# Attention that divides by sums standing on 16 rows of each head, without transposes

## The chip, the cores and the metric

The kernel runs on one core of one Trainium2 chip, as one launch. The metric is device time in microseconds (us); the time of a version is the median of its runs. The profile shows one execution of the program, taken by the hardware profiler.

## What is computed

The inputs are `x` and a context `ctx_1024`, each 8 batches x 256 tokens x 256 columns, float32. Four layers follow each other, each added to `x`:

```
x = x + autocorrelation_attention(layernorm(x), ctx, ctx)     # layer 0
x = x + expert_mlp_balanced(layernorm(x))                     # layer 0, 8 experts
x = x + cross_attention(layernorm(x), ctx)                    # layer 1
x = x + expert_mlp_top2(layernorm(x))                         # layer 1, 8 experts, 8 shared
```

The change is in the cross attention of layer 1, with 16 heads of 16 columns:

```
q  = (x @ Wq + bq).reshape(bs, n_ctx, 16, 16)
kv = (data @ Wkv + bkv).reshape(bs, n_data, 16, 32);  k, v = kv[..., :16], kv[..., 16:]
attn = softmax(einsum('bqhd,bkhd->bhqk', q, k) / 4, axis=-1)
out  = einsum('bhqk,bkhd->bqhd', attn, v).reshape(bs, n_ctx, 256) @ Wp + bp
```

The last layer's shared and routed experts are three products each, with a gate `silu(x @ w1) * (x @ w3)` and `@ w2`.

## The kernel before

The order of the instructions on each engine is the order of the Python code (a manual schedule); the engines run beside each other and meet at semaphores that the tile framework sets from the tiles' reads and writes. A tile of a pool with n buffers waits for the release of the tile n allocations earlier in the same pool and tag. PSUM has eight banks of 2 KB per row (512 float32).

`fast_path` holds the whole computation (a general path follows only if a flag is set). Its stages by the profile: layer 0 with its search for balanced experts and its products until about 214 us, the cross attention until about 343 us, overlapped at its end with the first block of the shared experts, then the expert blocks to the end.

**Before the attention.** `keys` and `vals` project the context. `vals` (L1414 to L1428) leaves the values in `VA`, 32 columns per head: 16 of values, then a column of ones and 15 of zeros, set by two POOL memsets (L1496, L1497). At L2467 to L2474 the rows of the output weights `wp` and of the value bias `bvc` are loaded in the order in which the heads will stand.

**The attention loop** (from L3019 on) goes over the 8 batches `b`, two steps `c` each; a step covers 8 heads, `4 g x 2 m`. In a step `scores(b, c, kt)` (L2666) makes, for each of two blocks `kt` of 128 keys, four 32-row matmuls over 512 columns into two tiles of `ps_s` (two banks each), and ScalarE writes the exponential to SBUF (L2681). `values` (L2685) of the step before multiplies `VA` with the exponentials: for each `g` and `m` a product of 32 rows (16 of values, one of sums) into `ps_v`, one bank, `[128, 2, 256]`. Then:

- `keep` (L2698) copies that bank to SBUF, `ov`, on VectorE.
- `turn_back(b)` (L2702) transposes `ov` back to tokens x columns on TensorE, 8 transposes a batch, takes the reciprocal of the sums, now one column per head, and multiplies: `on`.
- `turn_out(b)` (L2724) transposes `on` again, 4 transposes, and VectorE copies them to `oT`, the stationary operand of `project_out` (L2737).

Beside this run for other batches: `turn_q` (4 transposes of the normalised `x`, copied to `hT`), `queries` (L2633: products and two masked copies `QM`, one on ScalarE and one on VectorE), `add_y`, `batch_stats`, `norm_q`, `norm_m` (statistics on VectorE, their last steps on POOL), `take_apart_m` and `join_m` (ScalarE, with DMA transposes), and from batch 4 on `route`, the router of 512 tokens in eight pieces (L2844), whose small matmuls (logits `pl`, L2849; a transpose; counts behind `mk`, L2898 to L2903) use `ps_m`, and whose VectorE part is some thirty small operations. `send` issues the routed rows' indirect DMAs on POOL.

PSUM in this stage: `ps_m` three banks (transposes, queries, projection, router), `ps_s` two tiles of two banks, `ps_v` one bank.

**Behind the loop** (L3767 on) the last batch's `turn_back`, `turn_out` and `project_out` stand between the pieces of `classic_up` (the first block of the shared experts, L3248 to L3258) and of `route(2)`. At L3828 the banks are closed and new pools opened for the expert blocks: `Bs` two banks, `ps_a` two, `ps_e` two, `ps_m` and `ps_v` one each. `run_unit` then makes seven products per block with lists of VectorE steps (`early`, `amid`, `late`, `after`) put between them; `Rows.steps()` are four sums of the block's rows that the products need (tile `T`).

Of the kernel before, what the change touches and what calls it, by code (L numbers as in the profile page):

```python
# [9 lines left out]
F32 = mybir.dt.float32  # L10
BF16 = mybir.dt.bfloat16
U32, U16 = mybir.dt.uint32, mybir.dt.uint16
# [1074 lines left out]
def fast_path(  # L1087
# [261 lines left out]


    KT = pk.tile([P, NB, T], F32, name="KT")
    VA = pk.tile([P, NT, H, HW], F32, name="VA")
    WK = pst.tile([P, KC, H, DH], F32, name="WK")
    wkv = wkv_in.rearrange("p kc (h t d) -> p kc h t d", h=H, t=2)
    mask = pk.tile([P, 2], F32, name="mask")
# [59 lines left out]
    def vals(i, n, pool, copy=nc.scalar.copy):  # L1415
        pp = pool.tile([P, n, H, DH], F32, tag="pm", name="pp")
        for j in range(n):
            for kc in range(KC):
                nc.tensor.matmul(
                    pp[:, j],  # L1420
                    CT[:, kc, (i + j) * P : (i + j + 1) * P],
                    wkv[:, kc, :, 1, :],
                    start=(kc == 0),
                    stop=(kc == KC - 1),
                )
                if kc < KC - 1 or j < n - 1:
                    yield
        copy(VA[:, i : i + n, :, 0:DH], pp)  # L1428
        yield

    def in_steps(steps, n):
# [61 lines left out]
    )  # L1493
    bsel = pr.tile([P, NCT, 16], F32, name="bsel")
    nc.vector.tensor_copy(bsel, fold.to_broadcast([P, NCT, 16]))
    nc.gpsimd.memset(VA[:, :, :, DH:], 0.0)  # L1496
    nc.gpsimd.memset(VA[:, :, :, DH : DH + 1], 1.0)  # L1497

    spread = pa.tile([P, 2, 8, DH], F32, name="spread")
    nc.gpsimd.tensor_copy(  # L1500
# [963 lines left out]
    for e in range(E - 1):  # L2464
        if e == 5:

            wpv = L1_xattn_Wp.rearrange("(c g m d) n -> m g d c n", c=NB, g=4, m=2)  # L2467
            for m in range(2):
                for g in range(4):
                    r0 = 64 * m + DH * g  # L2470
                    nc.sync.dma_start(out=wp[r0 : r0 + DH], in_=wpv[m, g])
                    nc.sync.dma_start(
                        out=bvc[r0 : r0 + DH, :],
                        in_=bkv[:, 1, :].rearrange("(c g m) d -> m g d c", c=NB, g=4)[m, g],  # L2474
                    )
            nc.sync.dma_start(out=bpb, in_=L1_xattn_bp.partition_broadcast(P))
        search(
            e, rows.get(e), steps_of(e), *FILLS.get(e, (2.58, [2.58] * 4))
        )
        if e < 2:  # L2480
            for k, _ in enumerate(listers[e]):
                fill((1.29, 0.43, 1.72, 0.43)[k])
# [57 lines left out]
        nc.vector.tensor_tensor(X[:, h, :], X[:, h, :], py0[h], ALU.add)  # L2540
    l0.close()
    banks = ctx.enter_context(ExitStack())
    ps_m = banks.enter_context(tc.tile_pool(name="ps_m", bufs=3, space=PSUM))
    ps_s = banks.enter_context(tc.tile_pool(name="ps_s", bufs=2, space=PSUM))
    ps_v = banks.enter_context(tc.tile_pool(name="ps_v", bufs=1, space=PSUM))
    pq2 = at.enter_context(tc.tile_pool(name="pq2", bufs=2))
    py = at.enter_context(tc.tile_pool(name="py", bufs=2))
    warm = small.tile([P, 1], F32, tag="warm", name="warm")
# [11 lines left out]
    load_y(1)  # L2560
    load_y(2)

    QM, hTs, h2s, norms = {}, {}, {}, {}

    def add_y(b):
        xb = X[:, TPB * b : TPB * (b + 1), :]
# [65 lines left out]
    def queries(b, c, eng=nc.scalar):  # L2632
        if c == 0:  # L2633
            QM[b] = pq2.tile([P, NB, 2, S], F32, tag="QM", name="QM")
        pp = ps_m.tile([P, S], F32, tag="pm", name="pp")
        for kc in range(KC):
            nc.tensor.matmul(
                pp,
                wq[:, kc, c * P : (c + 1) * P],
                hTs[b][:, kc, :],  # L2640
                start=(kc == 0),
                stop=(kc == KC - 1),
            )
        for m in range(2):
            if m == 0 and eng is nc.scalar:
                nc.scalar.activation(
                    QM[b][:, c, m, :],
                    pp,
                    AF.Identity,
                    bias=bqm[:, c, m : m + 1],  # L2650
                    scale=mask[:, m : m + 1],
                )
            else:
                nc.vector.tensor_scalar(  # L2654
                    QM[b][:, c, m, :],
                    pp,
                    mask[:, m : m + 1],
                    bqm[:, c, m : m + 1],
                    ALU.mult,
                    ALU.add,  # L2660
                )

    pex = at.enter_context(tc.tile_pool(name="pex", bufs=4))
    ex, pvs, ovs, ons, oTs = {}, {}, {}, {}, {}

    def scores(b, c, kt):  # L2666
        k0 = b * S + kt * P
# [16 lines left out]

    def values(b, c, m):  # L2685
        if m == 0:
            pvs[b, c] = ps_v.tile([P, 2, S], F32, tag="pv", name="pv")
        for kt in range(TPB):
            for g in range(4):
                nc.tensor.matmul(  # L2690
                    pvs[b, c][32 * g : 32 * g + 32, m, :],
                    VA[:, b * TPB + kt, 8 * c + 2 * g + m, :],
                    ex[b, c, kt][:, g, m, :],
                    start=(kt == 0),
                    stop=(kt == TPB - 1),
                )

    def keep(b, c):  # L2698
        ovs[b, c] = pxs.tile([P, 2, S], F32, tag="ov", name="ov", bufs=3)
        nc.vector.tensor_copy(ovs[b, c], pvs.pop((b, c)))  # L2700

    def turn_back(b):  # L2702

        on = pxs.tile([P, TPB, NB, 2, 4, DH], F32, tag="on", name="on")
        ons[b] = on
        for qt in range(TPB):
            pt = ps_m.tile([P, NB, 2, 4, HW], F32, tag="pm", name="pt")
            for c in range(NB):
                for m in range(2):
                    nc.tensor.transpose(  # L2710
                        pt[:, c, m].rearrange("p g w -> p (g w)"),
                        ovs[b, c][:, m, qt * P : (qt + 1) * P],
                        ident,
                    )
            pv = pt.rearrange("p c m g w -> p (c m g) w")
            rs = small.tile([P, H, 1], F32, tag="rs", name="rs")
            nc.vector.reciprocal(rs, pv[:, :, DH : DH + 1])
            nc.vector.tensor_tensor(
                on[:, qt].rearrange("p c m g d -> p (c m g) d"),
                pv[:, :, 0:DH],  # L2720
                rs.to_broadcast([P, H, DH]),
                ALU.mult,
            )

    def turn_out(b):
        pt = ps_m.tile([P, NB, TPB, P], F32, tag="pm", name="pt")
        for c in range(NB):
            for qt in range(TPB):
                nc.tensor.transpose(
                    pt[:, c, qt, :],  # L2730
                    ons[b][:, qt, c].rearrange("p m g d -> p (m g d)"),
                    ident,
                )
        oTs[b] = pxs.tile([P, NB, TPB, P], F32, tag="oT", name="oT")
        nc.vector.tensor_copy(oTs[b], pt)

    def project_out(b):  # L2737
        pp = ps_m.tile([P, TPB, D], F32, tag="pm", name="pp")
        for qt in range(TPB):
            for c in range(NB):  # L2740
                nc.tensor.matmul(
                    pp[:, qt, :],
                    oTs[b][:, c, qt, :],
                    wp[:, c, :],
                    start=(c == 0),
                    stop=(c == NB - 1),
                )
# [270 lines left out]
    for b in range(B):  # L3018
        for c in range(NB):  # L3019
# [3 lines left out]
                norm_m(b - 2)  # L3023
            if (b, c) == (3, 0):
                router_weights()
            if prev:
                values(*prev, 0)
                values(*prev, 1)
                keep(*prev)
            send()  # L3030
            if prev is None:
                list(vals(4, 1, ps_m, nc.vector.tensor_copy))
            elif b == 0:
                turn_q(1)
            elif c == 0:
                if b + 1 < B:
                    turn_q(b + 1)
            else:
                turn_out(b - 1)
                if b >= 2:  # L3040
                    take_apart_m(b - 2)
            if c == 0 and b >= 3:
                join_m(b - 3)
            if gates:
# [12 lines left out]
                queries(1, 1, nc.vector)  # L3057
                norm_q(2, nc.vector, nc.vector)
            if c == 0:
                if b >= 1:  # L3060
                    turn_back(b - 1)
                if 0 < b and b + 1 < B:
                    queries(b + 1, 0)
                    queries(b + 1, 1)
# [701 lines left out]

    values(*prev, 0)  # L3767
    values(*prev, 1)
    keep(*prev)
    join_m(B - 3)  # L3770
    at.close()
    pe2 = ctx.enter_context(tc.tile_pool(name="pe2", bufs=2))
# [3 lines left out]
    acts0 = []  # L3776
    up0 = classic_up(WS[0], [HT[:, kc, 0:TB] for kc in range(KC)], acts0)
    next(up0)
    turn_back(B - 1)
    gate2 = route(2)  # L3780
    next(gate2)
    next(up0)
    turn_out(B - 1)
    next(gate2)
    next(up0)
    project_out(B - 1)
    batch_stats(B - 1, "m")
    norm_m(B - 1)
    send(2)
    next(gate2)  # L3790
    turn_m(B - 2)
    next(up0)
# [33 lines left out]
    for do in shared.steps(P, HF):  # L3826
# [5 lines left out]
        )  # L3832
        for i in range(2)
    ]
    ps_a = ctx.enter_context(tc.tile_pool(name="ps_a", bufs=2, space=PSUM))
    ps_e = ctx.enter_context(tc.tile_pool(name="ps_e", bufs=2, space=PSUM))
    ps_m = ctx.enter_context(tc.tile_pool(name="ps_m", bufs=1, space=PSUM))
    ps_v = ctx.enter_context(tc.tile_pool(name="ps_v", bufs=1, space=PSUM))

    for t in Bs:  # L3840
# [45 lines left out]
    for b in range(NBLK):  # L3886
# [24 lines left out]
        for k in range(1, NK):  # L3911
# [18 lines left out]
            if b == 1 and k == 3:  # L3930
                t = turned[n]
                early, amid = [lambda: t.join(0)], [lambda: t.join(1)]
                xs_[n] = Rows(t.RT)
                after = xs_[n].steps()
            if b == 2 and k == 1:
                amid = [lambda: t.join(0), lambda: t.join(1)]
                xs_[n] = Rows(t.RT)
            if b == 2 and k == 2:
                late = xs_[n].steps()
            run_unit(up_unit(b, k), early, amid, late, after)  # L3940
            if b == 1 and k == 1:
                Rs[3] = load_rows(1)
# [70 lines left out]
```

## Time and profile before

| | |
|---|---|
| median of 3 runs | 808.18 us (807.61 to 808.23) |
| the profiled execution | 807.99 us, span 806.3 us |
| TensorE matmuls busy | 790.3 us (98% of the span) |
| TensorE weight loads busy | 627.6 us (78%) |
| VectorE busy | 521.1 us (65%) |
| ScalarE busy | 369.6 us (46%) |
| POOL busy | 214.2 us (27%) |

The span runs from the first to the last instruction on the engines; 1.7 us of the execution's time lie around it. Busy is the union of an engine's instructions. TensorE's matmuls are pipelined and their ends are modelled, so its busy share is no measure of its peak; what counts is whether it waits. Shares are means over stages: VectorE's 65% says little about one stage, so stages are read in stretches of the timeline. An engine named before `<-` waits for the instruction named behind it. Shapes are rows x elements per row; `PEld` is the weight load, which overlaps matmuls.

### The profile page before, as it was taken

What the parts mean: (1) busy time and instruction counts of PE and PEld (TensorE: products, weight loads), DVE (VectorE), ACT (ScalarE), POOL (GpSimd) and SP (SyncE); (2) the same over time, 40 slices, a digit from 0 to 9 for tenths busy, and PEclk for the clock granted to TensorE, in tenths of its full rate; (3) what the DMA queues carried; (4) which work ended last, traced back from release to release, by engine and by line L of the source; (5) the groups of instructions that cost most, each with busy time, mean ns of one, the idle gap of its engine ahead of it and who ended that gap; (6) DMA issues with size and microseconds to landing.
All of it is one profiled execution on the core that took longest, in us unless ns stands there. A gap on an engine that the chain in (4) does not pass through costs nothing. (4 is left out here: it accounts for less than half of the span.)

```text
span 806.3 us, 13762 instructions
## 1 busy us (share of the span) xinstructions
PE 790.3 (98%) x5100; PEld 627.6 (78%) x5100; DVE 521.1 (65%) x1473; ACT 369.6 (46%) x676; POOL 214.2 (27%) x293
## 2 busy tenths in 40 slices
PE   7999999999999999999999999999999999999997
PEld 6547778788755555547898989798979898999996
DVE  6367887640466686456866686767676859686732
ACT  4344455234367777531425364444444535433430
POOL 6343122231126546543230001102122311112030
PEclk9999999999999999999999999999999999999999
DMA  8292666596161102161113585797759554411023
GB/s 267 78 307 86 218 202 174 191 269 224 53 182 30 27 16 59 41 210 60 56 55 100 170 243 156 190 298 197 196 137 296 111 179 112 122 14 20 8 30 132
DMA packets 111252, 111.16 MB, mean 138 GB/s; under 512 B 32936, under 2 KB 101768, under 8 KB 111144
## 3 DMA queue, kind: packets, MB, share of 16 engines
q1 hardware_dynamic: 102504, 96.87, 39.9%
q0 software_dynamic: 7920, 13.02, 7.6%
q8 instruction: 42, 0.69, 0.4%
q10 hardware_dynamic: 752, 0.30, 0.1%
q14 instruction: 34, 0.28, 0.1%
HBM read 80.61 MB, written 25.37 MB: 131 GB/s over the span
## 5 line engine op out<-in xcount | busy, mean ns | idle before, releaser
L3589 POOL DMA_INDIRECT Od<-Y,ids x32 | 50.7, 1584 | 285.1 <-DVE Y L3414 100.0
L3274 ACT COPY B<-a 128x512 f32<-128x512 f32 (+1 forms) x54 | 28.6, 531 | 168.2 <-PE a L3286 132.2
L2681 ACT ACTIVATE ex<-p,scale 128x1024 f32<-128x1024 f32 x64 | 67.8, 1110 | 25.3 <-PE p L2673 24.5
L3286 PE MATMUL a<-T,HP 128*128 128x256 f32 x288 | 73.9, 379 | 0.0
L3136 DVE TENSOR_TENSOR cc<-e,s 128x512 f32<-128x512 f32 x44 | 30.4, 691 | 57.1 <-PE e L3286 57.0
L3286 PE MATMUL a<-RT,wab 128*128 128x256 f32 x256 | 66.4, 382 | 0.4 <-DVE cc L3136 0.4
L3136 DVE TENSOR_TENSOR act<-act 128x256 f32<-128x256 f32 (+1 forms) x120 | 61.5, 513 | 2.7
L2385 PE MATMUL ph<-RT,w 128*128 128x256 f32 x256 | 62.0, 390 | 0.0
L2402 PE MATMUL py<-w,A 128*128 128x256 f32 x256 | 61.6, 387 | 0.0
L3286 PEld LDWEIGHTS a<-T,HP 128*128 128x128 f32 x288 | 54.0, 190 | 7.0
L3286 PEld LDWEIGHTS a<-RT,wab 128*128 128x128 f32 x256 | 46.5, 190 | 8.1 <-issue 1.6
L2385 PEld LDWEIGHTS ph<-RT,w 128*128 128x128 f32 x256 | 45.1, 190 | 8.0 <-ACT RT L2370 0.5
L2402 PEld LDWEIGHTS py<-w,A 128*128 128x128 f32 x256 | 46.3, 190 | 6.1
L2394 ACT ACTIVATE A<-ph,b1c 128x256 f32<-128x256 f32 x64 | 30.3, 474 | 43.7 <-PE ph L2385 36.7
L2944 POOL DMA_INDIRECT Td<-HP,to x32 | 32.6, 1017 | 59.5 <-DMA Td<-HP,to 54.1
L2673 PE MATMUL p<-QM,KT 32*128 32x512 f32 x256 | 41.0, 639 | 1.0 <-DVE QM L2654 0.5
L3136 DVE TENSOR_TENSOR act<-act,cc 128x512 f32<-128x512 f32 x44 | 30.3, 689 | 13.2 <-ACT act L3320 13.0
L2412 POOL DMA_INDIRECT Yd<-Y,ids x16 | 15.8, 988 | 74.5 <-DVE Y L2411 22.5
L3301 ACT COPY s<-a 128x512 f32<-128x512 f32 x44 | 25.8, 587 | 20.0 <-PE a L3286 20.0
L3286 PE MATMUL e<-T,wab 128*128 128x256 f32 x128 | 32.9, 380 | 0.3 <-DVE T L3136 0.3
L3136 DVE TENSOR_TENSOR cc<-a,s 128x512 f32<-128x512 f32 x44 | 30.4, 691 | 3.9
L3286 PE MATMUL B<-RT,wab 128*128 128x256 f32 x128 | 32.9, 379 | 0.0
(522 smaller groups left out, 1732.4 us busy)
## 6 DMA issues: line engine op xcount, KB each, us to landing
w<-in_L_ffn_w_dram SPq DMA_DIRECT2D x16, 1024.0 KB
wab<-in_L_ffn_w_e_dram SPq DMA_DIRECT2D x16, 1024.0 KB
wc<-in_L_ffn_w_e_dram SPq DMA_DIRECT2D x8, 1024.0 KB
sab<-in_L_ffn_w_e_dram SPq DMA_DIRECT2D x32, 256.0 KB
R<-Td SPq DMA_DIRECT2D x8, 530.0 KB
sc<-in_L_ffn_w_e_dram SPq DMA_DIRECT2D x16, 256.0 KB
Td<-blank SPq DMA_DIRECT2D x2, 1590.0 KB
X<-in_x_dram SPq DMA_DIRECT2D x4, 512.0 KB
```

What stands on the lines that cost most here:

```text
L2385: nc.tensor.matmul(ph, w1[:, kc, f * P : (f + 1) * P], RT[:, kc, :], start=(kc == 0), stop=(kc == KC - 1),)
L2394: nc.scalar.activation(A[:, f, :], ph, AF.Gelu_apprx_tanh, bias=b1c[:, e, f : f + 1])
L2402: nc.tensor.matmul(py, A[:, f, r * P : (r + 1) * P], w2[:, f, :], start=(f == 0), stop=(f == NF - 1),)
L2412: nc.gpsimd.indirect_dma_start(out=Yd, out_offset=bass.IndirectOffsetOnAxis(ap=ids[:, r : r + 1], axis=0), in_=Y[:, r, :], in_offset=None,)
L2673: nc.tensor.matmul(ps[g // 2][:, g % 2].rearrange("p m q -> p (m q)"), KT[rows, c, k0 : k0 + P], QM[b][rows, c].rearrange("p m q -> p (m q)"),
L2681: nc.scalar.activation(e4[:, 2 * j : 2 * j + 2], ps[j], AF.Exp, scale=scale)
L2944: nc.gpsimd.indirect_dma_start(out=Td, out_offset=bass.IndirectOffsetOnAxis(ap=to[g][:, k, j : j + 1], axis=0), in_=HP[:, GT * g + j, :], ...
L3136: eng.tensor_tensor(out, a, b, op)
L3274: nc.scalar.copy(self.b[:, 0 : self.n], self.a[:, 0 : self.n])
L3286: nc.tensor.matmul(ps[:, m * HT2 : (m + 1) * HT2], self.w.get(m, left, self.k), self.x.part[right], start=start and m == 0, stop=True, ski ...
L3301: nc.scalar.copy(self.s2, self.a)
L3589: nc.gpsimd.indirect_dma_start(out=Od, out_offset=bass.IndirectOffsetOnAxis(ap=ids, axis=0), in_=Y, in_offset=None, compute_op=ALU.add,)
```

## The change

`VA` keeps 32 columns per head, but now 16 of values and 16 of ones: for heads with `m = 0` the values stand first, for `m = 1` the ones. A product of 32 rows then leaves 16 rows of values and 16 equal rows of sums. `divide` replaces `keep`, `turn_back` and `turn_out`: it collects the sums of both halves into `den` (a copy, then a copy under the row mask `mask`), swaps the two halves of every 32 rows with a shuffle, takes the reciprocal, collects the values of both halves in PSUM under the other mask, and multiplies into `oT`, which is already columns x tokens. The order of `wp`'s and `bvc`'s rows follows.

The values' products move from `ps_v` to `ps_m`, which has two buffers instead of three; `ps_s` has three tiles of two banks instead of two; both query products of a batch share one tile. `turn_q(b + 1)` moves ahead of `values` in batches 1 to 6. Behind the loop the order of the pieces of `route(2)` and `classic_up` shifts by one, the new pools are opened in another order, and the row sums of two expert blocks are spread over other places.

```diff
-    VA = pk.tile([P, NT, H, HW], F32, name="VA")
+    VA = pk.tile([P, NT, H // 2, 4, DH], F32, name="VA")
...
-        copy(VA[:, i : i + n, :, 0:DH], pp)
+        copy(
+            VA[:, i : i + n, :, 0:4:3, :],
+            pp.rearrange("p n (g m) d -> p n g m d", m=2),
+        )
...
-    nc.gpsimd.memset(VA[:, :, :, DH:], 0.0)
-    nc.gpsimd.memset(VA[:, :, :, DH : DH + 1], 1.0)
+    nc.gpsimd.memset(VA[:, :, :, 1:3, :], 1.0)
...
-                    r0 = 64 * m + DH * g
+                    r0 = 2 * DH * g + DH * m
...
-    ps_m = banks.enter_context(tc.tile_pool(name="ps_m", bufs=3, space=PSUM))
-    ps_s = banks.enter_context(tc.tile_pool(name="ps_s", bufs=2, space=PSUM))
-    ps_v = banks.enter_context(tc.tile_pool(name="ps_v", bufs=1, space=PSUM))
+    ps_m = banks.enter_context(tc.tile_pool(name="ps_m", bufs=2, space=PSUM))
+    ps_s = banks.enter_context(tc.tile_pool(name="ps_s", bufs=3, space=PSUM))
...
-        pp = ps_m.tile([P, S], F32, tag="pm", name="pp")
+            pqs[b] = ps_m.tile([P, NB, S], F32, tag="pm", name="pp")
+        pp = pqs[b][:, c]
...
+    held = mask.bitcast(U32)
+    swap = list(range(DH, 2 * DH)) + list(range(DH))
...
-            pvs[b, c] = ps_v.tile([P, 2, S], F32, tag="pv", name="pv")
+            pvs[b, c] = ps_m.tile([P, 2, S], F32, tag="pm", name="pv")
...
-                    VA[:, b * TPB + kt, 8 * c + 2 * g + m, :],
+                    VA[:, b * TPB + kt, 4 * c + g, 2 * m : 2 * m + 2, :],
...
-    def keep(b, c):
-    def turn_back(b):
-    def turn_out(b):
...
+    def divide(b, c):
+        if c == 0:
+            oTs[b] = pxs.tile([P, NB, S], F32, tag="oT", name="oT")
+        pv = pvs.pop((b, c))
+        den = pxs.tile([P, S], F32, tag="den", name="den")
+
+        def upper(m):
+            return held[:, m : m + 1].to_broadcast([P, S])
+
+        nc.vector.tensor_copy(den, pv[:, 0])
+        nc.vector.copy_predicated(den, upper(0), pv[:, 1])
+        nc.vector.stream_shuffle(den, den, swap)
+        nc.vector.reciprocal(den, den)
+        nc.vector.copy_predicated(pv[:, 0], upper(1), pv[:, 1])
+        nc.vector.tensor_tensor(oTs[b][:, c], pv[:, 0], den, ALU.mult)
...
+            if c == 0 and 0 < b < B - 1:
+                turn_q(b + 1)
             if prev:
                 values(*prev, 0)
                 values(*prev, 1)
-                keep(*prev)
+                divide(*prev)
             send()
...
             elif b == 0:
                 turn_q(1)
-            elif c == 0:
-                if b + 1 < B:
-                    turn_q(b + 1)
-            else:
-                turn_out(b - 1)
-                if b >= 2:
-                    take_apart_m(b - 2)
+            elif c == 1 and b >= 2:
+                take_apart_m(b - 2)
...
-                if b >= 1:
-                    turn_back(b - 1)
...
-    turn_back(B - 1)
     gate2 = route(2)
-    next(gate2)
-    next(up0)
-    turn_out(B - 1)
     next(gate2)
     next(up0)
     project_out(B - 1)
     batch_stats(B - 1, "m")
     norm_m(B - 1)
     send(2)
+    next(gate2)
+    next(up0)
...
+    ps_m = ctx.enter_context(tc.tile_pool(name="ps_m", bufs=1, space=PSUM))
+    ps_e = ctx.enter_context(tc.tile_pool(name="ps_e", bufs=2, space=PSUM))
     ps_a = ctx.enter_context(tc.tile_pool(name="ps_a", bufs=2, space=PSUM))
-    ps_e = ctx.enter_context(tc.tile_pool(name="ps_e", bufs=2, space=PSUM))
-    ps_m = ctx.enter_context(tc.tile_pool(name="ps_m", bufs=1, space=PSUM))
...
-                after = xs_[n].steps()
+                sums = xs_[n].steps()
+                late, after = sums[:1], sums[1:]
...
             if b == 2 and k == 2:
-                late = xs_[n].steps()
+                sums = xs_[n].steps()
+            if b == 2 and k >= 2:
+                after = after + sums[2 * k - 4 : 2 * k - 2]
```

More of the change, by code (lines that the diff above doesn't have):

```diff
@@ L2561, in fast_path @@
     load_y(2)
-    QM, hTs, h2s, norms = {}, {}, {}, {}
+    QM, hTs, h2s, norms, pqs = {}, {}, {}, {}, {}
     def add_y(b):
@@ L2663, in fast_path @@
     pex = at.enter_context(tc.tile_pool(name="pex", bufs=4))
-    ex, pvs, ovs, ons, oTs = {}, {}, {}, {}, {}
+    ex, pvs, oTs = {}, {}, {}
+    held = mask.bitcast(U32)
+    swap = list(range(DH, 2 * DH)) + list(range(DH))
     def scores(b, c, kt):
@@ L2696, in values @@
                 )
-    def keep(b, c):
-        ovs[b, c] = pxs.tile([P, 2, S], F32, tag="ov", name="ov", bufs=3)
-        nc.vector.tensor_copy(ovs[b, c], pvs.pop((b, c)))
-    def turn_back(b):
[L2704 to L2723, printed above, removed]
-    def turn_out(b):
[L2726 to L2735, printed above, removed]
+    def divide(b, c):
[11 more added lines that the diff above has]
+        nc.vector.tensor_tensor(oTs[b][:, c], pv[:, 0], den, ALU.mult)
     def project_out(b):
@@ L2742, in project_out @@
                     pp[:, qt, :],
-                    oTs[b][:, c, qt, :],
+                    oTs[b][:, c, qt * P : (qt + 1) * P],
                     wp[:, c, :],
@@ L3768, in fast_path @@
     values(*prev, 1)
-    keep(*prev)
+    divide(*prev)
     join_m(B - 3)
```

## The prediction

> **What bounds the kernel now.** I read four views: the busy time by stretches (cut at the starts of the attention's value matmuls), the timelines of TensorE and VectorE over one batch, the groups by shape, and the waits inside the attention. The attention runs from about 220 to 343 us, one batch per two steps. Columns of the stretches: PE, PEld, DVE, ACT, POOL busy (instructions), granted clock, DMA.
>
> ```profile
> 245.91:260.18 14.27, 14.27 (x133) 8.09 (x131) 9.10 (x25) 10.44 (x12) 8.06 (x14) 1.00 0.17 37
> 260.18:274.38 14.20, 14.20 (x131) 7.95 (x129) 9.84 (x32) 11.48 (x13) 8.03 (x15) 1.00 0.16 40
> 289.29:304.69 15.40, 14.54 (x133) 8.10 (x131) 12.87 (x44) 11.57 (x13) 7.92 (x14) 1.00 0.09 19
> ```
>
> TensorE fills an ordinary batch (14.2 us) wholly; VectorE has 9.1 to 9.8 us of work, ScalarE 10.4 to 11.5. In the third stretch, where a router group runs beside the attention, VectorE already has 12.9 us. The waits inside the attention say the same: VectorE waits for matmuls.
>
> ```profile
> DVE ov L2700 <- PE pv L2690: 13.4, 11, 2.4
> DVE QM L2654 <- ACT QM L2646: 5.1, 10, 0.7
> DVE rs L2717 <- PE pt L2710: 4.6, 5, 0.9
> DVE X L2749 <- PE pp L2741: 4.6, 5, 1.2
> ```
>
> So a matmul removed here is worth its time only until VectorE has no more idle time.
>
> **What the change takes from TensorE.** One batch's steps, by TensorE's timeline (start, length):
>
> ```profile
> 263.70 1.09 PE L2710 MATMUL pt<-ident,ov 128*128 128x128 f32 x8
> 264.63 1.89 PE L2637 MATMUL pp<-hT,wq 128*128 128x256 f32 x8
> ...
> 269.39 0.65 PE L2729 MATMUL pt<-ident,on 128*128 128x128 f32 x4
> 269.97 1.14 PE L2673 MATMUL p<-QM,KT 32*128 32x512 f32 x8
> ```
>
> From start to next start the eight transposes of `turn_back` take 0.93 us and the four of `turn_out` 0.58: 1.51 us a batch, 12.1 us over eight. A third score buffer can also take the waits of scores for the exponential (3.0 us in ten waits). TensorE alone would then need 12.4 to 12.75 us an ordinary batch.
>
> **What it gives VectorE.** Groups by shape (busy us, mean ns), then the one reciprocal of a single column (ns, least, median, most):
>
> ```profile
> L2717 DVE RECIPROCAL rs<-pt 128x16 f32<-128x16 f32 x16 | 4.0, 251 | 4.6 <-PE pt L2710 4.6
> L2876 DVE RECIPROCAL rsm<-sm 128x4 f32<-128x4 f32 x4 | 0.7, 178 | 0.1
> L2718 DVE TENSOR_TENSOR on<-pt,rs 128x256 f32<-128x256 f32 x16 | 6.8, 425 | 0.6
> L2654 DVE TENSOR_SCALAR QM<-pp,mask,bqm 128x256 f32<-128x256 f32 x18 | 9.5, 542 | 8.4 <-ACT QM L2646 6.7 <-PE pp L2637 1.4
> ```
>
> ```profile
> L1803 DVE RECIPROCAL rtot<-es x1: 159/159/159, 35.8 to 35.8; 128x1 f32<-128x1 f32 x1
> ```
>
> The reciprocal is the step to watch. 1, 4 and 16 elements per row take 159, 178 and 251 ns: 6.3 and then 6.1 ns per element, six times a copy's pace. `divide` takes reciprocals of 256 columns on all rows, since each sum now stands on 16 rows: 153 + 256 x 6.1 = 1.71 us. Before, it was 2 x 16 columns a batch.
>
> Weighed against the Trainium skill, "VectorE: DVE Perf Modes", section "Walkthrough: the 8-slice pipeline in each mode": it says that reciprocal is an iterative divide with a repeat count of 8. Read as eight cycles per element at its 0.96 GHz, an estimate from that page gives 2.29 us, and the sum below would become about 825 us; the rows here have a smaller slope, and they decide.
>
> The other five operations of one `divide` are 128x256: a copy from PSUM (0.42), a predicated copy, a shuffle, another predicated copy (into PSUM), a multiply (0.425). Predicated copy and shuffle are in no row. They do not come free, since each streams 256 columns: from below 0.28 (the 128x128 copy of `lT`), from above 0.54 (`QM`). I take the 128x256 rows, 0.42, and 0.46 from start to next start where the next one needs the result (as between L3136 operations at 401.31 and 401.77). So one `divide` occupies VectorE for 4 x 0.46, 1.65 for the reciprocal (its next operation does not need it and starts 0.06 early) and 0.35 for the multiply: 3.84 us; with the ends for the three unknown ones, 3.4 to 4.2.
>
> Removed per batch, by starts: two `keep` copies (0.60 each), `turn_back`'s four operations (1.27), `turn_out`'s copy (0.60): 3.1 us. Added: 7.7. An ordinary batch then holds on VectorE: add of the projection 0.73, statistics 1.28, `hT` 0.60, two `QM` 0.92, `add_y` 0.71, statistics 1.29, `norm_q` 0.34, two divides 7.7: **13.5 us, above TensorE's 12.4 to 12.75**. VectorE becomes the bound; an ordinary batch gains 0.7 us instead of 1.5, and every router operation, hidden until now, is paid.
>
> **The sum.** Count VectorE's work from the first `divide` (where the first `keep` starts, 226.75) to the last one's start (now 333.55).
>
> - 15 divides x 3.84: 57.6.
> - Seven projection adds 5.1, six statistics 7.7, seven `hT` 4.2, sixteen `QM` 7.4, five `add_y` and statistics 10.0, eight `norm_q` 2.7, the router's columns 0.85, and two router groups at 0.2 + 0.4 + 2.6 + 1.9 + 1.0 = 6.1 each (starts 316.0 to 331): 12.2. Together 50.2.
> - Waits, laid out by hand in program order. (a) Start: `turn_q(1)`'s copy stands behind the first divide, so queries start at 231.2, not 228.3; `QM` waits 0.95, `hT(2)` 0.65, the second divide 1.3: 2.9. (b) `ps_m` now has two buffers, and the values take one of them: the router's logits, allocated behind the queries, must wait until the divide before them lets its bank go, and scores and values queue behind on TensorE. From its end 0.57 + 1.07 + 1.87 = 3.5 us pass until the next divide can start, in which VectorE has 3.1 us of work in batch 4 and 1.1 in batch 6: 0.4 + 2.4. (c) The counting matmuls wait for `mk`, which stands behind a divide on VectorE; behind them stand queries, scores and values: in batch 7 0.2 + 1.07 + 1.87 = 3.1 us, plus 0.3 of hand-overs, against 1.0 of VectorE's work: 2.4; in batch 5 queries come on top for both: 1.0. (d) 0.1 a batch for `values`, which waits for the projection's add to free its bank: 0.6. Together 9.7.
>
> 226.75 + 57.6 + 50.2 + 9.7 = 344.2 instead of 333.55: +10.7. Behind the loop, TensorE loses the last batch's transposes (0.93 + 0.58), and VectorE's last divide stands before L3258's first multiply, which then comes 3.6 us of TensorE later anyway: -1.5. In the expert blocks, two stalls of TensorE for row sums (0.34 at 443.48, 0.45 at 475.67) are where steps are split or moved: -0.8; if the moved sums only delay another step, nothing. The banks' new order after `banks.close()` stands at one wait of 0.51 (at 381.91), which can go or stay: 0 taken, 0.5 either way. One POOL memset (0.53) goes early, beside matmuls: nothing. Each moved DMA is issued as before.
>
> +10.7 - 1.5 - 0.8 = +8.4 on the profiled execution's 807.99 (span 806.3 and 1.7 around it): **816.4 us**. The median of the runs, 808.18, is 0.2 above that execution, inside what a measurement can tell (about 0.2%, 1.6 us).
>
> **Rivals.**
> 1. *TensorE stays the bound: faster.* If one `divide` takes 2.5 us (a reciprocal at a copy's 0.42), 15 x 1.3 us fall away, TensorE's 12.1 us are got, the late stalls too, less 1.6 at the start: 808.0 - 12.1 - 0.8 + 1.6 = 796.7. The mechanism is the reciprocal's pace in `divide`. It decides below 3.3 us per divide: there 15 x 0.54 us cancel the +8.4. The waits of the profile (VectorE idle for 31 us) speak for it, three rows of reciprocals against.
> 2. *VectorE is the bound, but the waits overlap.* With no wait at all the sum is -1.3: 806.7; with half of them 811.5. Against it: (a) follows from the order alone.
> 3. *Dearer divide or clock.* At 4.4 us per divide 15 x 0.56 more: about 825. Also, the clock was 0.55 from 41 to 44 us, behind a stretch in which TensorE was idle for 0.95 of 3.5 us; it stayed at 1.00 behind 0.77 of 3.4 us (214 to 217.4). TensorE will now wait over 1 us in several places; one such drop costs at most 1.7 us where TensorE is behind.
>
> That the change does not do what it says is excluded: its program has no `ov` or `on` transpose left, and sixteen chains of six operations in their place.
>
> **How the numbers follow.** Forecast, 812 to 821 (divide 3.55 to 4.1, waits 6 to 12): 0.56. Overlapping waits or a cheaper unknown operation, 807 to 812: 0.20. Dearer divide or clock, 821 to 830: 0.14. TensorE-bound, 795 to 805: 0.10. From 807 to 826 lie 0.56 + 0.20 + about 0.07 = 0.83. Faster by over 0.2% (below 806.6): the TensorE-bound case and 0.01 of error, 0.11; within (to 809.8): 0.09, out of the second case; slower: the rest, 0.80.
>
> **What would show it.** Sixteen reciprocals of 128x256 near 1.7 us each; VectorE's busy share above 90% from 230 to 343; TensorE waiting for `divide` (banks of `ps_m`) and for `mk`; the first `pgu` matmul of `classic_up` about 10 us later than 333.4; the expert blocks' length unchanged within 1 us. It is wrong if the reciprocal is near 0.4 us, or if TensorE is still above 97% busy between 245 and 330.

## The result and the profile after

The changed kernel takes **856.42 us** (855.11 to 858.44, 6 runs) against 808.2 for the kernel before on the same chip: ratio 1.060, 95% interval 1.0589 to 1.0614. The prediction was 816.4 us with a range of 807 to 826. The sign was right and the size was not: +48 us where +8 was worked out. The profiled execution took 858.12 us, span 856.3.

**Where the time went.** I cut both traces at the first value matmul of the attention and at the first `pgu` matmul of `classic_up` (columns as in the prediction: PE, PEld, DVE, ACT, POOL busy, granted clock, DMA share, GB/s). The attention of before, then that of after with two ordinary batches and one with a router group:

```profile
224.75:333.41 108.66, 107.19 (x1010) 59.34 (x1009) 72.97 (x220) 81.70 (x86) 56.33 (x98) 1.00 0.25 63
```

```profile
245.09:262.77 17.68, 14.88 (x118) 6.70 (x117) 12.44 (x27) 9.78 (x12) 3.14 (x14) 0.89 0.05 15
282.77:299.80 17.03, 14.41 (x117) 6.97 (x116) 12.09 (x26) 9.20 (x10) 6.01 (x11) 0.90 0.13 32
299.80:321.83 22.03, 16.80 (x134) 8.08 (x134) 17.37 (x48) 11.09 (x14) 8.71 (x15) 0.85 0.06 13
...
231.19:384.57 153.38, 117.50 (x925) 55.91 (x925) 105.77 (x272) 80.38 (x85) 57.28 (x100) 0.84 0.17 45
```

The attention starts 6.4 us later (231.19 against 224.75) and lasts 44.7 us longer; what follows it is 1.2 us shorter (471.7 against 472.9). That is the whole difference of 50.0 us in span. An ordinary batch takes 17.0 to 17.7 us instead of 14.2 (the one with the router's weights, from 262.77 on, 20.0), and the reader should look at the busy columns beside it: VectorE, which I had expected to be full, has 12.1 to 12.4 us of work in it, and TensorE 14.4 to 14.9. **No engine is full.** Over the stage TensorE idles for 35.9 us (1.5 before), VectorE for 47.6, and the granted clock is 0.84 where it was 1.00.

TensorE's account of the 44.7 us: the waits cost 34.4 (35.9 - 1.5). Its busy time rises by 10.3 although the transposes of the seven batches that lay in the stage before (7 x 1.51 = 10.6 us by starts) are gone, so its other work takes 20.9 us longer. (-10.6 + 20.9 + 34.4 = 44.7.) The clock is of the size to account for that: 16% of 153.4 us are 24.5 us of full-speed time not granted. That it accounts for all of it is not shown.

Picked from the waits of after between 220 and 400 us, those around TensorE's matmuls (engine, line, what it waited for; total, times, longest):

```profile
...
ACT QM L2648 <- PE pp L2639: 24.6, 9, 3.8
...
DVE QM L2656 <- ACT QM L2648: 20.6, 9, 2.8
DVE den L2713 <- PE pv L2694: 20.3, 12, 4.5
...
PE pp L2639 <- DVE QM L2656: 15.5, 8, 2.4
...
PE pc L2885 <- DVE mk L2881: 7.1, 2, 3.5
...
PE pp L2724 <- DVE mx L2852: 5.7, 2, 2.8
...
PE pp L2639 <- DVE hT L2623: 3.0, 1, 3.0
```

The three `QM` lines form a ring: TensorE's `pp` (a query product) waits for VectorE's `QM`, VectorE's `QM` for ScalarE's, ScalarE's for TensorE's `pp`. Before, `DVE QM <- ACT QM` was 5.1 us, at most 0.7 at a time, and TensorE's query products did not wait for `QM` at all. The timeline of after shows one turn of the ring (start, length, engine, instruction, and in brackets the idle time before it and what ended it):

```profile
247.33 0.42 DVE L2713 COPY den<-pv 128x256 f32<-128x256 f32 x1 [1.45 <-PE pv L2694]
...
248.26 1.13 PE L2639 MATMUL pp<-hT,wq 128*128 128x256 f32 x4
...
248.75 1.75 DVE L2716 RECIPROCAL den<-den 128x256 f32<-128x256 f32 x1
...
250.43 0.56 ACT L2648 ACTIVATE QM<-pp,bqm,mask 128x256 f32<-128x256 f32 x1
250.86 0.42 DVE L2718 TENSOR_TENSOR oT<-pv,den 128x256 f32<-128x256 f32 x1
251.20 0.54 DVE L2656 TENSOR_SCALAR QM<-pp,mask,bqm 128x256 f32<-128x256 f32 x1
251.79 1.47 PE L2639 MATMUL pp<-hT,wq 128*128 128x256 f32 x4 [2.41 <-DVE QM L2656]
253.20 2.09 PE L2677 MATMUL p<-QM,KT 32*128 32x512 f32 x8
253.30 0.56 ACT L2648 ACTIVATE QM<-pp,bqm,mask 128x256 f32<-128x256 f32 x1 [2.31 <-PE pp L2639]
253.90 0.54 DVE L2656 TENSOR_SCALAR QM<-pp,mask,bqm 128x256 f32<-128x256 f32 x1 [2.16 <-ACT QM L2648]
```

The first query product is done at 249.39. Its reader on VectorE stands behind the `divide` that began at 247.33, so it runs at 251.20. The second product lies in the same tile `pqs[b]`, hence waits for that reader, 2.41 us, and then VectorE, its `divide` done, waits 2.16 us for the second product. Each engine idles while the other works. The eight scores behind it take 2.09 us instead of the 1.14 of the trace before: the clock has dropped, to 0.63 in the stretch from 251.59 to 254.99.

### The profile page after: what moved, and what is told of

The parts are those of the page before. It is cut to its first block, busy times and chain, and to the rows that moved or that the text cites. A ratio compares the mean times of both kernels' runs of the same rounds, so it can differ in the third digit from the quotient of the medians.

```text
span 856.3 us, 13619 instructions
## 1 busy us (share of the span) xinstructions
PE 801.9 (94%) x5004; PEld 623.5 (73%) x5004; DVE 555.1 (65%) x1529; ACT 369.1 (43%) x676; POOL 214.9 (25%) x292
## 4 chain that ended last, share of the span: by engine, by line
PE 83%; DVE 11%; DMA 3%; POOL 1%; issue 1%; ACT 1%; ACTq 0%; SPq 0%; DVEq 0%; POOLq 0%
PE a L3264 18%; PE e L3264 9%; PE a L3323 8%; PE ph L2387 7%; PE py L2404 7%; PE B L3264 4%; PE e L3323 4%; PE pv L2694 4%; DVE den L2716 3%; PE py L3469 3%; PE pp L2639 2%; PE B L3323 2%; PE p L2677 2%; PE pp L1398 2%; PE pp L1419 2%; PE pgu L3226 1%
## 5 line engine op out<-in xcount | busy, mean ns | idle before, releaser
L2677 PE MATMUL p<-QM,KT 32*128 32x512 f32 x256 | 44.5, 767 | 0.0
L2639 PE MATMUL pp<-hT,wq 128*128 128x256 f32 x64 | 24.5, 520 | 19.6 <-DVE QM L2656 15.5
L3114 DVE TENSOR_TENSOR act<-act,cc 128x512 f32<-128x512 f32 x44 | 30.3, 689 | 13.3 <-ACT act L3298 13.1
L2694 PE MATMUL pv<-ex,VA 128*32 128x256 f32 x512 | 35.5, 424 | 2.5 <-DVE VA L1428 1.4
L2639 PEld LDWEIGHTS pp<-hT,wq 128*128 128x128 f32 x64 | 13.7, 237 | 30.0 <-DVE QM L2656 19.3
L2694 PEld LDWEIGHTS pv<-ex,VA 128*32 128x32 f32 x512 | 16.5, 120 | 25.5 <-issue 13.4
```

The lines of the kernel that those rows point to most:

```text
L2639: nc.tensor.matmul(pp, wq[:, kc, c * P : (c + 1) * P], hTs[b][:, kc, :], start=(kc == 0), stop=(kc == KC - 1),)
L2677: nc.tensor.matmul(ps[g // 2][:, g % 2].rearrange("p m q -> p (m q)"), KT[rows, c, k0 : k0 + P], QM[b][rows, c].rearrange("p m q -> p (m q)"),
L2694: nc.tensor.matmul(pvs[b, c][32 * g : 32 * g + 32, m, :], VA[:, b * TPB + kt, 4 * c + g, 2 * m : 2 * m + 2, :], ex[b, c, kt][:, g, m, :], ...
L3114: eng.tensor_tensor(out, a, b, op)
```

## Experiments

Theory A: the two query products share a tile, so the second waits for readers queued behind a `divide`; the waits, and the clock that drops with them, are the loss. Rival B: VectorE's load itself, the reciprocal above all, is the loss. Rival C: the banks taken from `ps_m` are. Twelve kernels were run. The stage columns are read like the stretches above, from first value matmul to first `pgu`, in each one's profiled execution.

| kernel | us (median) | ratio to before, 95% | stage, us | TensorE busy | VectorE busy | clock |
|---|---|---|---|---|---|---|
| before | 808.2 | 1 | 224.8 to 333.4 | 107.2 | 73.0 | 1.00 |
| after | 856.4 | 1.0589 to 1.0614 | 231.2 to 384.6 | 117.5 | 105.8 | 0.84 |
| m4_shared | 851.3 | 1.0521 to 1.0562 | 223.7 to 375.4 | 120.6 | 105.8 | 0.84 |
| split_only | 843.8 | 1.0411 to 1.0476 | 228.6 to 372.1 | 111.6 | 105.6 | 0.88 |
| m4 | 828.2 | 1.0238 to 1.0272 | 222.8 to 351.0 | 110.0 | 104.6 | 0.91 |
| m4_order | 815.8 | 1.0081 to 1.0128 | 223.0 to 340.3 | 104.3 | 103.2 | 0.94 |
| m4_order_act | 814.7 | 1.0088 to 1.0135 | 222.6 to 336.5 | 104.8 | 98.0 | 0.96 |
| m4_order_lnexp | 857.8 | 1.0607 to 1.0659 | 222.8 to 384.7 | 134.6 | 79.8 | 0.82 |
| qm_act | 857.3 | 1.0611 to 1.0647 | 224.8 to 374.8 | 115.8 | 99.6 | 0.85 |
| warm | 855.0 | 1.0594 to 1.0635 | 227.1 to 372.5 | 117.6 | 105.7 | 0.94 |
| shared_before | 818.4 | 1.0135 to 1.0169 | 224.0 to 343.1 | 108.8 | 73.5 | 1.00 |
| late_only | 804.9 | 0.9970 to 0.9987 | 223.1 to 331.7 | 107.1 | 73.0 | 1.00 |

(The kernel before took 806.3 to 806.6 beside the experiments, which ran on four chips, and 808.2 beside after; so a microsecond or two between rows says little. In the experiments' traces the work ahead of the attention also ends 0.3 to 2.1 us earlier than in that of before, so stages are compared by length.)

**m4** and **m4_shared**: four buffers for `ps_m` and two for `ps_s`; m4 also gives each query product a tile of its own.

```diff
-    ps_m = ...(name="ps_m", bufs=2, ...)
-    ps_s = ...(name="ps_s", bufs=3, ...)
+    ps_m = ...(name="ps_m", bufs=4, ...)
+    ps_s = ...(name="ps_s", bufs=2, ...)
...
# m4 alone:
-            pqs[b] = ps_m.tile([P, NB, S], F32, tag="pm", name="pp")
-        pp = pqs[b][:, c]
+        pp = ps_m.tile([P, S], F32, tag="pm", name="pp")
```

> Change with four buffers in ps_m, two score tiles (as before) and a query tile of its own for each c. Theory A (both query products in one bank: the second waits for VectorE's QM of the first, which stands behind divide, so TensorE and VectorE wait for each other, and the idle TensorE falls to half clock): the waits of L2639 for QM (15.5 us) and most half-clock windows (55 us of them) go; 815 to 825. Theory B (VectorE's 3.86 us per divide alone sets the length): stays above 845.

> Change with four buffers in ps_m and two score tiles, but both query products still in one tile. Theory A: the wait for QM stays (about 2.4 us in each of eight batches), 843 to 856. Theory C (the two buffers of ps_m, for which values, transposes, projection and router queue, are the cause): below 835.

Measured: 828.2 and 851.3 us. The buffers alone give back 5 us of the 48, the separate tiles 23 more. m4_shared is where A put it and far above C's 835; m4 is above the 815 to 825 expected, so something besides the ring is left. m4_shared still has `PE pp <- DVE QM` at 15.4 us; in m4 the line is gone, and both products run in one piece while VectorE is in the middle of a `divide`, as m4's timeline shows:

```profile
251.44 1.99 PE L2638 MATMUL pp<-hT,wq 128*128 128x256 f32 x8
251.45 0.01 DVE L2714 LOAD_MASK_SELECT den<-den  x1
251.45 0.43 DVE L2714 STREAM_SHUFFLE den<-den 128x256 f32<-128x256 f32 x1
251.92 1.75 DVE L2715 RECIPROCAL den<-den 128x256 f32<-128x256 f32 x1
```

**qm_act**: the reader that stands behind `divide` goes to the other engine.

```diff
-            if m == 0 and eng is nc.scalar:
+            if eng is nc.scalar:
```

> Change with both masked copies QM on ScalarE from batch 2 on, so that no query product waits for VectorE. Theory A: the second product waits 1.1 us for ScalarE instead of a divide; 820 to 832. Theory B: VectorE only loses 16 x 0.46 us; about 849.

Measured: 857.3 us, a clear miss. The waits of its trace tell why, and ScalarE's timeline at one of them:

```profile
PE pp L2639 <- ACT QM L2648: 11.5, 6, 2.1
PE pc L2885 <- DVE mk L2881: 7.1, 2, 3.5
...
259.33 2.12 ACT L2685 ACTIVATE ex<-p,scale 128x1024 f32<-128x1024 f32 x2 [2.14 <-PE p L2677]
261.33 1.02 ACT L2648 ACTIVATE QM<-pp,bqm,mask 128x256 f32<-128x256 f32 x2
```

The second product now waits for ScalarE's reading, which stands behind two exponentials of 1.11 us each. So my theory was too narrow: a reader of the shared tile in ScalarE's queue holds the second product up as well as one in VectorE's.

**split_only**: separate query tiles, two buffers (the edit of m4's second hunk alone).

> The changed kernel with each query product in a tile of its own, the two buffers of ps_m and three score buffers kept. Theory A (TensorE waits wherever a bank's reader stands in a queue behind a divide): with two buffers the second product now needs the bank of the value product before it, which only the divide lets go, so the wait changes its name and stays: 845 to 860 us. Rival (the shared tile alone is at fault, as the 23 us between the two four-buffer kernels would say if the two edits added up): 830 to 838 us.

Measured: 843.8 us, between the two expectations. The waits decide:

```profile
PE pp L2638 <- DVE oT L2717: 9.6, 5, 2.0
PE pc L2884 <- DVE mk L2880: 7.1, 2, 3.5
```

As A said, the wait changed its name: `oT` is the last operation of `divide`, which lets the bank of the value product go. It became 6 us smaller, not zero. The two edits do not add up: separate tiles bring 12.6 us with two buffers and 23.1 with four, four buffers bring 5.1 with a shared tile and 15.6 without.

**shared_before**: the kernel before with one line of the change, the shared query tile; the transposes and the short `keep` copies stay.

```diff
-        pp = ps_m.tile([P, S], F32, tag="pm", name="pp")
+            pqs[b] = ps_m.tile([P, NB, S], F32, tag="pm", name="pp")
+        pp = pqs[b][:, c]
```

> The kernel before with one edit: both query products of a batch in one tile of ps_m (three buffers kept, transposes and keep copies kept). Theory A (sharing costs what stands ahead of the tile's readers on VectorE and ScalarE): TensorE waits about 0.6 to 1.5 us in each of eight batches, no half clock above 7 us: 812 to 820 us. Rival 1 (sharing costs its 23 us whatever stands on VectorE): 828 to 834 us. Rival 2 (sharing costs nothing without the divides): 806 to 809 us.

Measured: 818.4 us, as A expected. No wide reciprocal, no buffer fewer, a granted clock of 1.00, and 12 us are gone. This is the edit that I had not priced at all. The waits that the trace before had smaller (5.1 and 1.8 us) or, the last, not at all:

```profile
DVE QM L2655 <- ACT QM L2647: 15.1, 12, 1.8
...
ACT QM L2647 <- PE pp L2638: 11.8, 7, 1.8
...
PE pp L2638 <- DVE QM L2655: 9.2, 7, 1.4
```

**m4_order**: m4 with `divide` issued later in the step, behind the router's next piece and `turn_q`'s copy.

```diff
-                divide(*prev)
             send()
...
+            if prev:
+                divide(*prev)
```

> The version with four ps_m buffers, with divide issued on VectorE behind the router's next piece and behind the first turn_q's copy instead of ahead of them. The waits of the counting matmuls for mk (7.1 us in two) and of the first queries for hT (3.0) go, and with them half-clock windows: 812 to 822. If divide only moves the delay to the projection: 826 to 830.

Measured: 815.8 us. An ordinary batch takes 13.6 to 14.7 us (value matmuls at 240.75, 254.66, 268.29, 282.99), the wait for `hT` is gone, that for `mk` still 5.0 us. Here the stage comes near to what I had predicted for after, with VectorE busy for 103.2 of 117.3 us:

```profile
223.02:340.32 117.30, 104.25 (x927) 54.33 (x925) 103.24 (x273) 80.17 (x85) 55.92 (x98) 0.94 0.22 58
```

**m4_order_act**: the same with both readers of the query products on ScalarE (the edit of qm_act).

> The kernel with four buffers, separate query tiles and the later divide, with both mask products of the queries on ScalarE instead of one on each. Theory A (VectorE is the bound there): 8 x 0.46 us leave VectorE, 811 to 815 us. Rival (the products queue behind exponentials on ScalarE, as in the kernel with shared tiles, and the scores wait): 818 to 826 us.

Measured: 814.7 us (811.21 to 816.94), inside A's range at its upper end, and not to be told from m4_order: the intervals overlap. 5.2 us left VectorE's work in the stage; the median shows 1. So it is not shown that VectorE's work sets m4_order's time. With tiles of their own the products do not suffer from ScalarE's queue, where qm_act's did.

**no_recip** and **m4_const**: after without the reciprocal, and m4 with the reciprocal replaced by an operation at a copy's pace (a constant in place of the quotient). Both leave the division out. Behind the fast path their traces then have the general one, which runs only when the flag is set: 3535 and 3514 us in all. These totals cannot be held against the expectations; the attention stage can.

> Change without the reciprocal (the product is with the sums, not their inverses). VectorE loses 16 x 1.67 = 27 us. Theory A: the QM wait shrinks from 2.4 to about 0.8 us a batch and most half-clock windows go; 808 to 818, still not faster than before. Theory B: 829. If TensorE were the bound without it: 797.

> The version with four ps_m buffers (828), with the reciprocal replaced by one multiply-add that writes 1/290 (the quotient is left out). VectorE loses 16 x about 1.35 us = 21. Theory B (once the query products have a bank each, VectorE's length is the bound): 800 to 808, with little half clock. If other waits bound it (order of router and divide): 815 or more.

The stage lasts 128.3 us without the reciprocal (after: 153.4) and 113.4 with the cheap operation (m4: 128.2; before: 108.7). So the reciprocal's length counts for 25.1 us of after's stage and 14.8 of m4's, about as much as the shared tile and the two buffers do: 25.2 with the reciprocal, 14.9 without it. They enlarge each other: behind the reciprocal stand the tile's readers, as the turn of the ring above shows. Without any reciprocal the shared tile and the two buffers still leave the stage 19.6 us longer than before, with `PE pp <- DVE QM` at 13.3 us; B alone does not carry the loss. But A's forecast for no_recip failed: the wait is still 1.9 us a batch and not 0.8, and by an estimate from the stages (856.4 - 25.1) the kernel would take about 831 us, near B's 829 and above A's 808 to 818. For m4_const the same estimate gives 813 us, between its two cases.

**m4_order_lnexp**: the reciprocal as exp(-ln) on ScalarE, which keeps the quotient.

```diff
-        nc.vector.reciprocal(den, den)
+        nc.scalar.activation(den, den, AF.Ln)
+        nc.scalar.activation(den, den, AF.Exp, scale=-1.0)
```

> The kernel with four buffers, separate query tiles and the later divide, with the reciprocal of the sums made on ScalarE as exp(-ln) (two activations of 128x256) instead of on VectorE. Sixteen times 1.75 us leave VectorE, about 3.3 us a batch; ScalarE gets some 1.9 us a batch. Theory A (what is left of the loss there is VectorE's load): VectorE falls to 10.2 us a batch, TensorE bounds at 12.4 to 12.8: 800 to 810 us. Rival (the two activations queue behind exponentials of 1.11 us, and VectorE stands in the middle of a divide until they are done): 812 to 825 us. If ScalarE has to change its table for each logarithm, more than 825 us.

Measured: 857.8 us, the third case. ScalarE's groups between 220 and 390 us:

```profile
L2715 ACT ACT_TABLE_LOAD x16 | 20.5, 1283 | 0.3
L2716 ACT ACT_TABLE_LOAD x16 | 20.5, 1283 | 0.3
L2715 ACT ACTIVATE den<-den 128x256 f32<-128x256 f32 x16 | 6.7, 416 | 22.9 <-DVE den L2714 21.4 <-DVE den L2713 1.5
```

Each logarithm loads a table and each exponential behind it loads the other: 41.1 us in 32 loads, and VectorE stands in the middle of `divide` for them, 30.7 us (`DVE oT <- ACT den`). It does not tell what a cheap division would be worth.

**warm**: after with the scores of the second key tile issued twice, which is idle work for TensorE against the falling clock.

```diff
-            nc.tensor.matmul(
+            for _ in range(1 + kt):
+                nc.tensor.matmul(
...
```

> Change as it is, but the four score matmuls of the second key block are issued twice (the same products into the same place), 16 x 1.07 = 17 us more work for TensorE, put where it idles anyway. Theory A with the clock (idle TensorE falls to half clock, and its half-speed products lie on the chain): fewer than 25 us of half clock instead of 55, and no slower than the change: 840 to 855. Without a part of the clock: 856 plus some of the 17 us, 860 to 870.

Measured: 855.0 us (845.73 to 858.49). It is at the upper end of what the theory with the clock expected and below the 860 of the other case. 128 more matmuls, about 18 us at the 1.14 us of eight, cost nothing. In the profiled execution (845.73 us) the clock is 0.94 instead of 0.84, TensorE's busy time the same 117.6 us, and the stage 8 us shorter. The other executions of this one program go with the clock too: 851.5 us at a mean of 0.985 over the whole span, 855.0 at 0.980, 855.5 at 0.976, and the profiled one 0.989. That speaks for the clock as part of the loss and not only its shadow, but the median is after's within the intervals; how much of the 48 us a steady clock alone would bring stays open.

**late_only**: the kernel before with only the row sums of the two expert blocks spread as in the change.

```diff
-                after = xs_[n].steps()
+                sums = xs_[n].steps()
+                late, after = sums[:1], sums[1:]
...
-                late = xs_[n].steps()
+                sums = xs_[n].steps()
+            if b == 2 and k >= 2:
+                after = after + sums[2 * k - 4 : 2 * k - 2]
```

> The kernel before with nothing but the row sums of two expert blocks spread as in the change. The prediction had two stalls of 0.34 and 0.45 us go: 0.5 to 1.0 us faster. If the moved sums delay other steps: no difference.

Measured: 804.9 us, ratio 0.9979 (0.9970 to 0.9987). From the seventh group of `pgu` matmuls to the end the trace has 442.16 us instead of 442.88, and TensorE's waits of 0.34 and 0.45 us are gone. This part of the change is a small gain, 0.2%; the trace places 0.7 of its 1.6 us, the rest is not located.

## Why the prediction was wrong

- **TensorE's 1.51 us a batch** went as said as far as the program goes: no transposes are left, and in the kernels whose clock was higher, m4_order and m4_order_act, TensorE is busy for 104 to 105 us of the stage at clocks of 0.94 and 0.96, against 107.2 before at 1.00. In after an ordinary batch holds 14.4 to 14.9 us of TensorE's work, not 12.4 to 12.75, at a granted clock of 0.89 to 0.90.
- **The price of one `divide`**, 3.84 us, was right. In after it goes from 233.20 to 237.06, 3.86 us. The groups by shape, of which two had no row before:

```profile
L2716 DVE RECIPROCAL den<-den 128x256 f32<-128x256 f32 x16 | 28.0, 1753 | 0.6
L2714 DVE COPY_PREDICATED den<-mask,pv 128x256 f32<-128x256 uint32 x16 | 7.1, 443 | 0.5
L2715 DVE STREAM_SHUFFLE den<-den 128x256 f32<-128x256 f32 x16 | 7.0, 437 | 0.0
```

  1.75 us for 256 columns against 1.71 from the slope of three small rows; the eight cycles per element that I had read into the repeat count of 8 in the Trainium skill ("VectorE: DVE Perf Modes", section "Walkthrough: the 8-slice pipeline in each mode") would have been 2.29.
- **VectorE's work** was right too: 57.6 + 50.2 = 107.8 us by starts, against 105.5 busy from the first `divide` to the first `pgu`.
- **The waits, 9.7 us, are the step that failed.** The last `divide` starts at 384.7; from 226.75, with 107.8 us of work, that leaves 50.1 us of VectorE's waits; part of the clock lost by TensorE lies in them. Those I had named are there: (a) for `hT` behind the first `divide` (3.0, where I had 2.9), for `mk` (7.1 us of TensorE's time, two waits of 3.5, where I had 2.4 and 1.0 net), and for a bank of the router (5.7 in two; the projection waits for `mx`, where I had the logits waiting and 2.8 net). Two others stood in no term.

  The first lies ahead of the first `divide`: the stage starts 6.4 us late, and 6.1 of them arise behind L2532 (L2534 in after), the last product ahead of the values' projection. There the products of `vals` and the transposes wait for ScalarE's copies to `VA`, and the second query product for the readers of the first:

```profile
213.61 1.99 PE L1419 MATMUL pp<-wkv_in,CT 128*128 128x256 f32 x8 [0.68 <-ACT VA L1428]
216.28 0.66 PE L2620 MATMUL pt<-ident,h 128*128 128x128 f32 x4 [0.68 <-ACT VA L1428]
...
221.20 2.08 PE L2639 MATMUL pp<-hT,wq 128*128 128x256 f32 x4 [1.37 <-DVE QM L2656]
```

  With four buffers and the shared tile (m4_shared) 1.1 us of the 6.1 are left, with separate tiles besides (m4) nothing. So the two buffers cost 5.0 us here, and that is most of what four buffers alone gave back.

  The second is the largest: the shared tile. What I had laid out in program order was the queue of each engine, and I had read the shared tile `pqs[b]` in the diff as a saving of banks. I had put both products at 1.87 us in one piece, as in the trace of before. They come in two pieces, with a reading by VectorE and ScalarE between them, in every batch. Alone on the kernel before this costs 12 us (shared_before), and beside the divides 12.6 to 23.1, by the number of buffers.
- **"VectorE is the bound"** failed with it: its busy share from 233 to 385 us is 70% (105.5 of 151.4), not above 90%. The signs that I had named for being wrong (a reciprocal near 0.4 us, TensorE above 97% busy) did not come either: none of them watched the waits. m4_order comes nearest, with 88%, and its 815.8 us stand beside my 816.4. That the sum priced a kernel without the ring is a hint and no proof, and the nearness is partly luck: m4_order has four buffers, another place for `divide`, a clock of 0.94 and the wait for `mk` at 5.0 us, and taking 5.2 us from VectorE there brought 1 (m4_order_act).
- **"One such drop costs at most 1.7 us"** was right in size for most of them; I had seen one coming. Read in stretches of 3.4 us from 231.19 on, the granted clock of after falls in ten places. In seven of them two neighbouring stretches show some 0.65 and 0.85, which is 1.7 us of full-speed time not granted; in three the clock stays at 0.50 for a stretch or two, and they cost 3.4, 5.1 and 3.4. Together that is 24 us, fourteen times 1.7. I had noted that TensorE would wait over 1 us in several places and that 0.95 of 3.5 us had been enough, and did not multiply.
- **Behind the loop** -1.5 and -0.8 were predicted, and -1.2 came in all. Of TensorE's three waits of the expert blocks (0.51, 0.34, 0.45) only the first is left in after. TensorE's busy time there fell by the 1.5 (466.8 to 465.3), but its other idle time rose by 1.1, which I did not price and which is not traced further. `banks.close()` at 0, and POOL's memset at nothing, were not tried alone.
- **The rivals.** The reciprocal at a copy's pace would not have made after faster than before: without any reciprocal its stage is still 19.6 us longer (no_recip). "The waits overlap" went the wrong way: there are 50 us of them and not less than 9.7. A dearer `divide` did not occur, a lost clock did, at more than ten times its price.

By the kernels in one order the 49.9 us between before and after (806.5 to 856.4) are: VectorE's load and what goes with it 9.3 (m4_order), the place of `divide` 12.4 (m4), the shared query tile 23.1 (m4_shared), two buffers for four 5.1. In another order the parts are other ones, as split_only and the stages without the reciprocal show; each contains the clock that was lost with it.

The clock is also where the Trainium skill had the warning. "TensorE: Matmul & The Clock Gate", section "A second HAM failure mode: psum-queue depth-cycling", tells of a kernel that cycles through PSUM banks and idles briefly between groups of matmuls often enough for the clock to swing between half and full rate. That agrees with this trace: waits of 1 to 3.5 us between groups, a granted clock between 0.50 and 1.00 in stretches of 3.4 us, and 0.84 over the stage.

## What to carry to other kernels

Price a merged tile like a moved instruction: write down who writes it, who reads it, and what stands ahead of each reader in its queue, since two products in one tile have to take turns with their readers. When a long operation enters an in-order engine, follow every short reading that now stands behind it to the engine that waits for its bank; a sum of busy times can be right to 2% and the total wrong by 40 us. Count TensorE's waits of over a microsecond, and if there are several per stage, price the clock over the whole stage.

## What the runs showed of the hardware

- The granted clock fell with TensorE busy at 77% of the stage (117.5 of 153.4), in waits of at most 3.5 us; at 91% with waits up to 1.4 us (shared_before, 108.8 of 119.1) it stayed at 1.00. At 92% with waits up to 3.0 us (m4_order_act, 104.8 of 113.9) it was 0.96, so the busy share alone does not tell these stages apart.
- A copy under a mask of 128x256 took 0.44 us from PSUM to SBUF and 0.41 into PSUM, a shuffle of rows 0.44 with 0.01 for its mask: the pace of a copy (0.425). The reciprocal took 1.75.
- A change between logarithm and exponential on ScalarE took 1.283 us each time, both ways.
